# Deformable convolution and expert convolution: first offsets worked out in the head, the experts' products grouped, their neighbour rows on 64 partitions

## The chip, the cores and the metric

One core of one Trainium2 chip. The metric is the device time of one execution in microseconds, the median of several. The kernel is written in a tile language whose pools hand out buffers and insert the waits; the order of instructions on each engine is the order of the program text (a manual schedule).

## The reference

Two residual layers on x of shape (2, 256, 128, 128), float32. `_gn` normalises over 32 groups of 8 channels.

```python
def _L0(x):   # deformable 3x3 convolution, 256 -> 256 channels, here cut
    offset = conv3x3(x, w_off) + b_off          # 18 channels: dy, dx of 9 taps
    mask = sigmoid(conv3x3(x, w_mask) + b_mask) # 9 channels
    py, px = base_y + dy, base_x + dx           # for each output pixel and tap
    sampled = bilinear(x, py, px) * mask        # zero outside the image
    return einsum('bckhw,ock->bohw', sampled, w_conv) + b_conv

def _L1(x):   # 8 experts of rank 8
    h = conv(x, weight_in)     # 1x3 along a row, 256 -> 8 for each expert
    o = conv(h, weight_out)    # 3x1 down a column, 8 -> 256
    return einsum('e,ebchw->bchw', probs, o)

x = x + _L0(_gn(x))
x = x + _L1(_gn(x))
```

The eight experts together are one convolution to 64 channels (ER), a scaling by probs, and one convolution back.

## The kernel before

The normalised image is stored in DRAM as a table: one cell per pixel holds the 256 channels of the pixel and of the one below, 2 KB, with a border of zeros. A sample of one row of 128 pixels and one tap (a *unit*) is one indirect DMA of 4 KB per partition, two neighbouring cells, so all four corners at once. An image is 16 groups (`NG`) of 8 rows (`GR`), each of two chunks of 4 rows (`CR`), 9 taps: 72 units per group, 1152 per image, 2304 in all.

**Head.** x of image 0 is loaded in 16 tiles `xa` (SP queue), with `bn_stats` on VectorE as they land; then the small weights `bias`, `wu` and `bcv` are loaded. `norm_pieces` makes mean, `rstd` and `shift` (with two small matmuls by `gavg`). In a loop over the groups, `head_norm` normalises `xa` in place on ScalarE and VectorE, `transposes` turns it on TensorE, ScalarE and VectorE copy the result to `hpx` (two buffers), and `store_cells` stores 8 rows of cells, 2 MB. After the last group `offset_pieces` prepares, from rstd and shift, the scaled weights `wus` and the constant part `at` that let the offset convolution run on the raw x. Then the large weights follow on the SP queue: `wcv` (2.3 MB, L314), `win` (L315), six parts of `wout` (L319), two of `pr` (L321).

**The stream.** Everything after is laid out in *slots*, one unit each. `sched[slot]` holds the pieces that are put beside the units, and a loop over the slots emits, in this order: `gather` of unit s+15 (POOL, L491, 15 buffers), `product` of unit s+3 (ScalarE, L501: first corner times its weight into `acc`, 9 buffers), `add` of the other three corners (VectorE, L507), `apply_tap` of s-8 (TensorE, L532: one 128x512 product into `po`), `turn` of s-1 (TensorE, L517: two transposes to `ptr`), `keep` (ScalarE, L525: to `sm`), then the pieces of the slot.

The pieces are: `load_x`; `offsets_of(b, g, at_slot)`, which works out the offsets of a group from 83 slots ahead of it (`row_of` L369 into `pu`, `keep_rows` L379, `shifted` L391 into `om`, ten small VectorE steps up to `cidx` and `wt`; it reads the raw `x` tiles of its group and the next); `table_beside(1)`, which builds image 1's table beside image 0's units; and, beside image 1's units, `experts` for image 0. When a chunk's last tap is applied, `residual` (L541) adds `po` to the x tile, `result_stats` (L545) takes statistics, and `store_x1` (L548) stores the group.

For group 0 of image 0 the 83 slots lie ahead of the first unit, so `load_x`, the offset products and the small steps all come before the first gather.

**The experts.** `experts` handles 32 chunks of 4 rows. For chunk ci it loads `xc` one step ahead (L618), normalises it (`xcn`, L623) and makes `ph` on TensorE (`hidden`, L641): for each of 6 combinations of channel half and tap, one product for even rows into partitions 0 to 63 and one for odd rows into 64 to 127. These six pieces are put two slots apart. `scale` (L648) copies `ph` times probs to `h`, so that a partition half of `h` is a parity of rows. `back` (L667) then makes the 256 output channels: for each of two channel halves m six products of 128 partitions into `pe`. A product with `wout` 0 or 2 takes both row parities, two taps at once, 256 columns; the third tap lies in the row pair beside, so `wout` 1 and 3, zero in one partition half, take 128 columns each. They are put two to a slot. `total` (L676) adds `xc`, and `store` writes the output (L679). The step is 34 slots per chunk, beside image 1 and also in the *tail*, where `experts` runs for image 1 with nothing beside it. `ph`, both `pe`, `pu` and `om` share three PSUM buffers, `p_m`.

One product of float32 appears in the trace as two matmul instructions.

Of the kernel before, what the change touches and what calls it, by code (L numbers as in the profile page):

```python
# [34 lines left out]
P = 128  # L35
# [10 lines left out]
GR = 8  # L46
# [21 lines left out]
def layers(ctx, tc, x, w_om, b_om, w_cv, b_cv, w_in, w_out, probs, out):  # L68
# [45 lines left out]
    nc.vector.tensor_copy(base, base_i)  # L114

# [71 lines left out]
    def store_cells(b, j, px):  # L187

        pairs = bass.AP(
            px.tensor, px.offset, [px.ap[0], [C, GR], [1, CELL]]  # L190
        )
        nc.sync.dma_start(cells(b, GR * j - 1, GR), pairs)
# [7 lines left out]
    def offset_pieces(norm, psum, tag, name):  # L200
        mean, rstd, shift = norm
        wus = cp.tile([P, NH, NU], F32, name=f"wus_{name}")
        at = [cp.tile([P, GR, NO], F32, name=f"at{i}_{name}") for i in range(3)]
        spread = cp.tile([P, NH, P], F32, name=f"spread_{name}")
        nb = cp.tile([P, NU], F32, name=f"nb_{name}")
        by_row = cp.tile([P, 3, NO], F32, name=f"by_row_{name}")
# [52 lines left out]
    norms0, offs = [None] * B, [None] * B  # L259


    with ExitStack() as s:
        hx = s.enter_context(tc.tile_pool(name="hx", bufs=NG))
        hp = s.enter_context(tc.tile_pool(name="hpx", bufs=2))
        hs = s.enter_context(tc.tile_pool(name="hstat", bufs=1))
        ht = s.enter_context(tc.tile_pool(name="hpt", bufs=6, space=PSUM))
        h1 = s.enter_context(tc.tile_pool(name="hp1", bufs=1, space=PSUM))
        stats = hs.tile([P, NH, NCH, 6], F32, name="hstats")
        xv = view(x, 0)
        xs = []  # L270
        for g in range(NG):
            xt = hx.tile([P, NH, GN], F32, tag="hx", name=f"xa_{g}")
            nc.sync.dma_start(xt, xv[:, :, g * GN : (g + 1) * GN])
            xs.append(xt)
            for i in range(CPG):
                for h in range(NH):
                    nc.vector.bn_stats(stats[:, h, g * CPG + i], xt[:, h, i * N : (i + 1) * N])
        nc.sync.dma_start(bias, b_om.partition_broadcast(P))
        nc.sync.dma_start(wu, w_om.rearrange("p h x o -> p h (x o)"))
        nc.sync.dma_start(bcv, b_cv)  # L280
        norms0[0], pieces = norm_pieces(stats, hs, h1, "g", "0_0")
        for piece in pieces:
            piece()
        mean, rstd, shift = norms0[0]

        def head_norm(g):
            nc.scalar.activation(
                xs[g][:, 0], xs[g][:, 0], AF.Identity, bias=shift[:, 0:1], scale=rstd[:, 0:1]
            )
            nc.vector.tensor_scalar(  # L290
                xs[g][:, 1], xs[g][:, 1], mean[:, 1:2], rstd[:, 1:2], ALU.subtract, ALU.mult
            )

        px, last = None, None
        head_norm(0)
        for g in range(NG):
            px = hp.tile([P, GR + 1, C], F32, tag="hp", name=f"hpx_{g}")
            nc.gpsimd.tensor_copy(px[:, 0], last[:, GR] if g else zero[:, :C])  # L298
            if g + 1 < NG:
                head_norm(g + 1)  # L300
            for i in range(0, GR, 2):
                ps = ht.tile([P, 2, C], F32, tag="t", name=f"hpt_{g}_{i}")
                transposes(ps, xs[g], (i, i + 1))
                if i % 4 == 0:
                    nc.scalar.copy(px[:, 1 + i : 3 + i], ps)
                else:
                    nc.vector.tensor_copy(px[:, 1 + i : 3 + i], ps)
            store_cells(0, g, px)
            last = px
        store_last(0, last)  # L310
        offs[0], pieces = offset_pieces(norms0[0], h1, "g", "0")
        for piece in pieces:
            piece()
        nc.sync.dma_start(wcv, w_cv)  # L314
        nc.sync.dma_start(win, w_in)  # L315
        for i, (even, odd) in enumerate(((1, 2), (None, 0), (0, 1), (2, None))):
            for half, t in enumerate((even, odd)):
                if t is not None:
                    nc.sync.dma_start(wout[half * ER : (half + 1) * ER, i], w_out[:, t])  # L319
        for half in range(2):  # L320
            nc.sync.dma_start(pr[half * ER : (half + 1) * ER], probs)  # L321


# [3 lines left out]
    xp = pool(ctx, "x", 3)  # L327
    up = pool(ctx, "u", 1)
    ip = pool(ctx, "idx", 2)
    gp = pool(ctx, "gather", GA)  # L330
    ap = pool(ctx, "acc", 9)
    sp = pool(ctx, "sampled", 3)
    st = pool(ctx, "stat", 1)
    p_o = pool(ctx, "p_o", 1, space=PSUM)
    p_t = pool(ctx, "p_t", 3, space=PSUM)
    p_m = pool(ctx, "p_m", 3, space=PSUM)
    sides = ExitStack()
    ctx.enter_context(sides)

    sched = defaultdict(list)  # L340

    def put(slot, piece):
        sched[slot].append(piece)

    xts = {}

    def load_x(b, g):
        xt = xp.tile([P, NH, GN], F32, tag="xt", name=f"x_{b}_{g}")
        nc.sync.dma_start(xt, view(x, b)[:, :, g * GN : (g + 1) * GN])
        xts[b, g] = xt  # L350
# [4 lines left out]
    def offsets_of(b, g, at_slot):  # L355
# [4 lines left out]
        def row_of(j, i):  # L360

            if i == 0:
                held["ps", j] = p_m.tile([P, 2, C], F32, tag="m", name=f"pu_{nm}_{j}")
            y = y0 - 1 + 2 * j + i
            if not 0 <= y < H:
                return
            xt, r = xts[b, y // GR], y % GR
            for h in range(NH):
                nc.tensor.matmul(  # L369
                    held["ps", j][:, i, :NU], lhsT=xt[:, h, r * W : (r + 1) * W],  # L370
                    rhs=offs[b][0][:, h], start=(h == 0), stop=(h == NH - 1),
                )
# [28 lines left out]
        def s_pos():  # L401
            om = held["om"][:, : GR * NO].rearrange("p (r o) -> p r o", o=NO)
            at = offs[b][1][0 if g == 0 else 2 if g == NG - 1 else 1]
            nc.vector.tensor_tensor(t("pm", [P, GR, NO]), om, at, ALU.add)
# [55 lines left out]
        rows_at = [8 * j for j in range(4)] + [38]  # L460
        for j in range(5):
            put(at_slot + rows_at[j], lambda j=j: row_of(j, 0))
            put(at_slot + rows_at[j] + 3, lambda j=j: row_of(j, 1))
            put(at_slot + rows_at[j] + 6, lambda j=j: keep_rows(j))
        for n in range(9):
            put(at_slot + 45 + n, lambda n=n: shifted(n))
        put(at_slot + 55, s_pos)
        put(at_slot + 56, s_mask)
        small = (s_clamp_y, s_clamp_x, s_round, s_low, s_far, s_near, s_cell, s_index, s_masked, s_weights)
        for n, piece in enumerate(small):  # L470
            put(at_slot + 56 + n, piece)
# [79 lines left out]
    def table_beside(b):  # L551
# [40 lines left out]
        offs[b], pieces = offset_pieces(norms0[b], p_m, "m", str(b))  # L592
# [3 lines left out]
        for j in range(NG):  # L596
# [7 lines left out]
            put(slot + 42, lambda j=j: store_cells(b, j, held["px", j]))  # L604
# [215 lines left out]
```

## Time and profile before

| | us |
|---|---|
| median of 3 runs | 3915.23 (3913.02 to 3915.41) |
| the profiled execution | 3914.82 |
| its span, first to last instruction | 3912.8 |
| head, until the first `product` | 193.1 |
| tail, from the last aggregation of statistics (3677.9) | 234.9 |

| engine | busy us | share |
|---|---|---|
| TensorE, matmul (PE) | 3565.9 | 91% |
| TensorE, weight load (PEld) | 1978.3 | 51% |
| VectorE (DVE) | 3401.8 | 87% |
| ScalarE (ACT) | 1952.9 | 50% |
| GpSimd (POOL) | 2347.6 | 60% |

DMA moved 1469.56 MB, 376 GB/s on average, 1208.11 MB of it by the gathers.

In the profile's lines a line number is that of the kernel above, `out<-in` names tiles without their numbers, `xN` counts instructions, and the bracket at the end of a timeline line is how long the engine was idle before and what ended that. SP is the queue that issues ordinary DMAs. Ends of matmuls are modelled and overlap; their starts are what a cost is read from.

### The profile page before, as it was taken

The page shows a single profiled execution, that of the slowest core. Times are in us where ns is not written, and L with a number is a line of the kernel's source. Part 1 is how long each engine was busy: PE and PEld are TensorE (multiplying, and loading weights), DVE is VectorE, ACT ScalarE, POOL GpSimd, SP SyncE. Part 2 cuts the span into 40 slices and gives each one's busy share as a digit, 9 for nine tenths or more (in the row PEclk, how much of TensorE's full clock was granted, in tenths as well). Part 3 has the DMA queues.
Part 4 walks back from the last instruction along what each step waited for, and adds up shares of the span by engine and source line. Part 5 has one row for each costly group of instructions (what it writes and reads, how often), then busy time and mean ns, then how long its engine had stood idle before and what let it go on. Part 6 is the DMA issues. An engine that isn't in the chain of part 4 may idle for free.

```text
span 3912.8 us, 53037 instructions
## 1 busy us (share of the span) xinstructions
PE 3565.9 (91%) x14684; PEld 1978.3 (51%) x14684; DVE 3401.8 (87%) x7905; ACT 1952.9 (50%) x3995; POOL 2347.6 (60%) x2334
## 2 busy tenths in 40 slices
PE   2588898998888989898999999999999999999899
PEld 2444444554444544444445555555555555554576
DVE  6299999998988989899999999999999999999512
ACT  1254445555555555565555555555555555555322
POOL 0076666666666666666767666666666666667100
PEclk8699999999999999999999999999999999999999
DMA  8899999999999999999999999999999999999544
GB/s 325 322 405 409 401 389 383 389 410 407 399 412 409 397 412 401 410 406 396 408 397 397 394 397 397 389 383 375 385 381 398 399 393 395 392 395 376 194 151 146
DMA packets 433977, 1469.56 MB, mean 376 GB/s; under 512 B 41982, under 2 KB 43134, under 8 KB 433556
## 3 DMA queue, kind: packets, MB, share of 16 engines
q0 software_dynamic: 331776, 1208.11, 78.7%
q1 hardware_dynamic: 100496, 255.41, 17.3%
q8 instruction: 119, 1.95, 0.2%
q10 hardware_dynamic: 1412, 2.67, 0.2%
q14 instruction: 174, 1.43, 0.1%
HBM read 1328.61 MB, written 137.41 MB: 375 GB/s over the span
## 4 chain that ended last, share of the span: by engine, by line
PE 44%; DMA 26%; DVE 20%; issue 7%; ACT 2%; SPq 0%; POOL 0%; ACTq 0%; DVEq 0%; POOLq 0%
PE po L532 24%; DMA g<-table,cidx 21%; DVE acc L507 16%; PE ptr L517 6%; PE ph L641 4%; PE pe L667 4%; PE pu L369 4%; DMA table<-hpx 2%; DMA xc<-x 2%; PE om L391 1%; DVE stats L545 1%; DVE x L541 1%; ACT acc L501 1%; DVE tstats L563 1%; DMA table<-zero 1%
## 5 line engine op out<-in xcount | busy, mean ns | idle before, releaser
L507 DVE SCALAR_TENSOR_TENSOR acc<-g,wt,acc 128x256 f32<-128x256 f32 x6912 | 3008.2, 481 | 171.9 <-ACT acc L501 84.4
L491 POOL DMA_INDIRECT g<-table,cidx x2304 | 2337.1, 1014 | 1162.8 <-DVE acc L507 403.3
L532 PE MATMUL po<-sm,wcv 128*128 128x512 f32 x4608 | 2404.9, 604 | 120.2 <-ACT sm L525 69.1
L501 ACT ACTIVATE acc<-g,wt 128x256 f32<-128x256 f32 x2304 | 1106.4, 506 | 555.3 <-DMA g<-table,cidx 455.0
L517 PEld LDWEIGHTS ptr<-idp,acc 128*128 128x128 f32 x4608 | 613.4, 142 | 1440.1 <-issue 773.3
L525 ACT COPY sm<-ptr 128x512 f32<-128x512 f32 x1152 | 667.3, 579 | 1064.7 <-PE ptr L517 1062.3
L517 PE MATMUL ptr<-idp,acc 128*128 128x128 f32 x4608 | 906.1, 279 | 84.7 <-DVE acc L507 53.9
L532 PEld LDWEIGHTS po<-sm,wcv 128*128 128x128 f32 x4608 | 739.0, 191 | 231.6 <-ACT sm L525 84.0
L369 PE MATMUL pu<-wus,x 128*128 128x243 f32 x1264 | 315.6, 374 | 18.2 <-DMA x<-in_x_dram 18.2
L667 PE MATMUL pe<-h,wout 128*128 128x128 f32 (+1 forms) x1520 | 261.5, 312 | 0.0
L676 DVE TENSOR_TENSOR xo<-pe,xc 128x512 f32<-128x512 f32 x128 | 87.9, 687 | 189.2 <-PE pe L667 189.2
L369 PEld LDWEIGHTS pu<-wus,x 128*128 128x128 f32 x1264 | 221.4, 194 | 29.3 <-issue 17.9
L641 PE MATMUL ph<-xcn,win 128*64 128x254 f32 (+1 forms) x1536 | 220.9, 398 | 13.7 <-ACT xcn L623 12.6
L667 PEld LDWEIGHTS pe<-h,wout 128*128 128x128 f32 x1520 | 220.7, 191 | 24.9 <-issue 14.2
L391 PE MATMUL om<-u,idp 128*128 128x216 f32 (+1 forms) x576 | 154.7, 352 | 6.1 <-ACT u L379 6.1
L623 ACT ACTIVATE xcn<-xc,shift,rstd 128x512 f32<-128x512 f32 x128 | 100.8, 811 | 70.3 <-DMA xc<-x 70.3
L641 PEld LDWEIGHTS ph<-xcn,win 128*64 128x64 f32 x1536 | 89.3, 137 | 87.3 <-issue 39.3
L541 DVE SCALAR_TENSOR_TENSOR x<-po,bcv,x 128x512 f32<-128x512 f32 x128 | 95.5, 746 | 32.5 <-PE po L532 32.5
L379 ACT COPY u<-pu 128x486 f32<-128x486 f32 (+1 forms) x160 | 87.5, 547 | 34.6 <-PE pu L369 34.6
L391 PEld LDWEIGHTS om<-u,idp 128*128 128x128 f32 x576 | 88.3, 193 | 8.1 <-ACT u L379 8.1
L545 DVE BATCH_NORM_STATS2 stats<-x 128x6 f32<-128x512 f32 x128 | 87.6, 684 | 0.1
L298 POOL COPY hpx<-hpx 128x256 f32<-128x256 f32 x15 | 6.5, 435 | 133.7 <-DMA table<-hpx 73.6
(78 smaller groups left out, 590.2 us busy)
## 6 DMA issues: line engine op xcount, KB each, us to landing
g<-table,cidx POOLq DMA_INDIRECT x2304, 9.2
table<-hpx SPq DMA_DIRECT2D x16, 2048.0 KB, 9.3
x<-in_x_dram SPq DMA_DIRECT2D x32, 1024.0 KB, 9.7
x<-x SPq DMA_DIRECT2D x32, 1024.0 KB, 9.3
table<-tpx SPq DMA_DIRECT2D x16, 2048.0 KB, 18.7
xc<-x SPq DMA_DIRECT2D x64, 512.0 KB, 5.4
out_dram<-xo SPq DMA_DIRECT2D x64, 512.0 KB, 6.5
xa<-in_x_dram SPq DMA_DIRECT2D x16, 1024.0 KB, 10.6
```

What stands on the lines that cost most here:

```text
L369: nc.tensor.matmul(held["ps", j][:, i, :NU], lhsT=xt[:, h, r * W : (r + 1) * W], rhs=offs[b][0][:, h], start=(h == 0), stop=(h == NH - 1),)
L391: nc.tensor.matmul(om[:, lo:hi], lhsT=idp[:, tx : tx + P], rhs=held["u"][:, ty + lo : ty + hi, col : col + NO], start=(ty == 1 and tx == 1 ...
L491: nc.gpsimd.indirect_dma_start(out=gt[:], out_offset=None, in_=tables[b][:, :], in_offset=bass.IndirectOffsetOnAxis(ap=idx[:, rr, k : k + ...
L501: nc.scalar.activation(acc, gts[u][:, 0:C], AF.Copy, scale=wt[:, 0, rr, k : k + 1])
L507: nc.vector.scalar_tensor_tensor(accs[u], gt[:, q * C : (q + 1) * C], wt[:, q, rr, k : k + 1], accs[u], ALU.mult, ALU.add)
L517: nc.tensor.transpose(pts[u // 2][:, h, (r % 2) * W : (r % 2 + 1) * W], acc[:, h * P : (h + 1) * P], ident)
L525: nc.scalar.copy(sms[u // CR][:, :, (r - 1) * W : (r + 1) * W], pts.pop(u // 2))
L532: nc.tensor.matmul(pos_[b, ci, m], lhsT=wcv[:, h, k, m * P : (m + 1) * P], rhs=sms[u // CR][:, h], start=(k == 0 and h == 0), stop=(k == K ...
L541: nc.vector.scalar_tensor_tensor(v, pos_.pop((b, ci, m)), bcv[:, m : m + 1], v, ALU.add, ALU.add)
L545: nc.vector.bn_stats(stats1[b][:, m, ci], xts[b, ci // CPG][:, m, at_ : at_ + N])
L641: nc.tensor.matmul(o[:, :, to], lhsT=win[:, h, tap], rhs=rows[:, t, :, of], start=(n == 0), stop=(n == 5),)
L667: nc.tensor.matmul(ps[m].rearrange("p (j t x) -> p t j x", t=2, x=W)[:, t, to], lhsT=l, rhs=hs[c].rearrange("p (j x) -> p j x", x=W)[:, of ...
```

## The change

Five parts.

1. **Group 0's offsets in the head.** `offsets_of` now returns its pieces with their slots. For group 0 of image 0 it is given the normalised tiles `xs`, the unscaled weights `wu` and a constant `plain` (base and bias), which need nothing of `offset_pieces`. Its 36 pieces are run four at a time after the stores of groups 2 to 10 of the head's loop. `load_x` and `offset_pieces` stay, after the loop, for the groups that follow.
2. **Weights earlier.** `wcv`, `win`, `wout` and `pr` are loaded right after `bcv`, ahead of the norm.
3. **First stores.** In group 0 of the head, cells are stored two rows at a time, as soon as they are copied. The transposes have four PSUM buffers in place of six, since `p_m` exists from the head on.
4. **The experts.** All 12 products of `hidden` come in one slot. `back` makes the 128-partition products of both row parities (t) into two PSUM tiles, each holding both channel halves. `back_beside` makes the eight neighbour products in one slot, with 64 partitions of `wout` and `h` in place of 128 with zeros: t = 0 reads partitions 64 to 127, t = 1 reads 0 to 63, in turns. `total` goes by t, with rows interleaved. The step is 33 slots beside image 1.
5. **The tail.** All pools of the stream are closed first; the experts then have 8 PSUM buffers and 8, 3, 4 and 4 of `xc`, `xcn`, `h` and `xo`. Pieces are ordered with a step of 24, and `xc` is loaded six chunks ahead.

```diff
-        ht = s.enter_context(tc.tile_pool(name="hpt", bufs=6, space=PSUM))
+        ht = s.enter_context(tc.tile_pool(name="hpt", bufs=4, space=PSUM))
...
         nc.sync.dma_start(bcv, b_cv)
+        nc.sync.dma_start(wcv, w_cv)
+        nc.sync.dma_start(win, w_in)
+        for i, (even, odd) in enumerate(((1, 2), (None, 0), (0, 1), (2, None))):
...
+        nc.vector.tensor_tensor(
+            plain, base, bias.unsqueeze(1).broadcast_to([P, GR, NO]), ALU.add
+        )
+
+        samples = [piece for _, piece in offsets_of(0, 0, (xs, wu, plain))]
...
-            store_cells(0, g, px)
+                if g == 0:
+                    store_cells(0, g, px, i, 2)
+            if g > 0:
+                store_cells(0, g, px, 0, GR)
+            if g > 1:
+                for piece in samples[:4]:
+                    piece()
+                del samples[:4]
...
-        def hidden(ci, n):
+        def hidden(ci):
+
+            ps["h"] = psum.tile([P, 512], F32, tag=tag, name=f"ph_{b}_{ci}")
+            for n, (h, tap) in enumerate(((0, 1), (1, 1), (0, 0), (1, 0), (0, 2), (1, 2))):
...
+        def back(ci, m):
+
+            for t in range(2):
+                if m == 0:
+                    ps[t] = psum.tile([P, NH, N // 2], F32, tag=tag, name=f"pe_{b}_{ci}_{t}")
+                nc.tensor.matmul(
+                    ps[t][:, m], lhsT=wout[:, 2 * t, m * P : (m + 1) * P], rhs=hs[ci],
+                    start=(m == 0), stop=False,
+                )
+
+        def back_beside(ci):
+            last = {0: 1, 1: 1 if ci + 1 < NCH else 0}
+            for m in range(NH):
+                for j in range(2):
+                    for t, c, i in ((0, ci - 1 + j, 1 - j), (1, ci + j, 1 - j)):
+                        if not 0 <= c < NCH:
+                            continue
+                        half = slice(ER, P) if t == 0 else slice(0, ER)
+                        nc.tensor.matmul(
+                            ps[t][:, m, j * W : (j + 1) * W],
+                            lhsT=wout[half, 1 + 2 * t, m * P : (m + 1) * P],
+                            rhs=hs[c][half, i * W : (i + 1) * W],
+                            start=False, stop=(m == NH - 1 and j == last[t]),
+                        )
...
         for ci in range(NCH + 1):
             e = first + step * ci
             if ci < NCH:
-                put_(e - step, lambda ci=ci: load(ci))
+                put_(e - ahead, lambda ci=ci: load(ci))
...
-                for n in range(6):
-                    put_(e + 5 + 2 * n, lambda ci=ci, n=n: hidden(ci, n))
-                put_(e + 18, lambda ci=ci: scale(ci))
+                put_(e + 6, lambda ci=ci: hidden(ci))
+                put_(e + 9, lambda ci=ci: scale(ci))
             if ci > 0:
                 c = ci - 1
                 for m in range(NH):
-                    n_parts = len(parts(c, m))
-                    for n in range(n_parts):
-                        put_(e + 20 + 5 * m + n // 2, lambda c=c, m=m, n=n: back(c, m, n))
-                    put_(e + 27 + 5 * m, lambda c=c, m=m: total(c, m))
-                put_(e + 33, lambda c=c: store(c))
+                    put_(e + 12 + 3 * m, lambda c=c, m=m: back(c, m))
+                put_(e + 18, lambda c=c: back_beside(c))
+                for t in range(2):
+                    put_(e + 20 + 2 * t, lambda c=c, t=t: total(c, t))
+                put_(e + 23, lambda c=c: store(c))
...
-        pools = expert_pools(sides, 0)
-        experts(0, norms1[0], pools, p_m, "m", put, slot + 36, 34)
+        pools = expert_pools(sides, 3, 2, 4, 2)
+        experts(0, norms1[0], pools, p_m, "m", put, slot + 36, 33, 33)
...
-    sides.close()
-    pools = expert_pools(sides, 0)
+    stream.close()
+    p_m = pool(ctx, "p_e", 8, space=PSUM)
+    pools = expert_pools(ctx, 8, 3, 4, 4)
     tail = defaultdict(list)
-    experts(1, norms1[1], pools, p_m, "m", lambda slot, piece: tail[slot].append(piece), 0, 34)
+    experts(1, norms1[1], pools, p_m, "e", lambda slot, piece: tail[slot].append(piece), 0, 24, 24 * 6)
```

## The prediction

> **What bounds the kernel now.** I read the stage table first (columns: span, then busy time and count of PE, PEld, DVE, ACT, POOL, then granted TensorE clock, DMA share, GB/s).
>
> ```profile
> 160.00:165.00 5.00, 0.00 (x0) 0.00 (x0) 0.00 (x0) 0.00 (x0) 0.00 (x0) 0.50 0.72 227
> 185.00:190.00 5.00, 3.75 (x19) 3.15 (x17) 2.72 (x11) 0.83 (x2) 1.16 (x1) 1.00 0.00 0
> ...
> 2014.00:2114.00 100.00, 94.18 (x356) 48.37 (x356) 97.44 (x233) 53.72 (x116) 71.13 (x71) 1.00 1.02 402
> 3014.00:3114.00 100.00, 100.00 (x422) 56.61 (x421) 96.03 (x226) 53.26 (x114) 68.11 (x68) 1.00 1.02 399
> ...
> 3700.00:3800.00 100.00, 95.98 (x696) 72.50 (x695) 20.05 (x29) 28.20 (x43) 0.00 (x0) 1.00 0.49 154
> ```
>
> Four regimes. Until 155 us the head is bound by the table stores (DMA share 1.03, 380 GB/s). From 155 to 193 us a chain of latencies runs with DMA partly empty. The stream follows; in its second image, beside the experts, PE is at 98.6% (mean of 1914 to 3614 us), DVE at 95.0%. The last 235 us (the tail) are PE alone. The timeline of the head's end:
>
> ```profile
> 164.28 1.10 SPq L321 DMA_DIRECT2D pr<-in_probs_dram  x2
> 165.50 1.03 SPq L349 DMA_DIRECT2D x<-in_x_dram  x2
> ...
> 171.05 10.28 PE L369 MATMUL pu<-wus,x 128*128 128x243 f32 x36 [17.76 <-DMA x<-in_x_dram]
> ...
> 188.00 0.46 DVE L453 TENSOR_TENSOR wt<-nf 128x288 f32<-128x288 f32 x1
> 188.62 1.16 POOL L491 DMA_INDIRECT g<-table,cidx  x1 [43.49 <-DVE wt L453]
> ...
> 193.12 0.51 ACT L501 ACTIVATE acc<-g,wt 128x256 f32<-128x256 f32 x1 [5.35 <-DMA g<-table,cidx]
> ```
>
> SP issues the weights before it issues x; PE waits for x, and POOL for the indices. Then PE's timeline inside the second image, to price an expert piece:
>
> ```profile
> 2730.02 0.38 PE L517 MATMUL ptr<-idp,acc 128*128 128x128 f32 x2
> 2730.24 1.02 PE L532 MATMUL po<-sm,wcv 128*128 128x512 f32 x2
> 2731.09 0.38 PE L517 MATMUL ptr<-idp,acc 128*128 128x128 f32 x2
> 2731.41 0.65 PE L641 MATMUL ph<-xcn,win 128*64 128x256 f32 x4
> 2731.99 1.13 PE L532 MATMUL po<-sm,wcv 128*128 128x512 f32 x2
> 2732.95 0.38 PE L517 MATMUL ptr<-idp,acc 128*128 128x128 f32 x2
> ```
>
> Starts tell the cost, since ends overlap. A unit (ptr and po) takes 2731.09 - 2730.02 = 1.07 us; one with a `hidden` piece 2732.95 - 2731.09 = 1.86. The piece costs 0.78 us. Consecutive 512-column instructions start 0.43 us apart, so 256 columns stream in 0.213 and 128 in 0.107. The piece's four instructions of 256 columns, on two 64-column halves, therefore overlap in pairs (0.43 us), and 0.35 is the change of array shape, there and back. The tail, one chunk:
>
> ```profile
> 3748.62 3.78 PE L667 MATMUL pe<-h,wout 128*128 128x256 f32 x24
> ...
> 3752.32 2.80 PE L641 MATMUL ph<-xcn,win 128*64 128x256 f32 x24
> ...
> 3755.05 3.78 PE L667 MATMUL pe<-h,wout 128*128 128x256 f32 x24
> ...
> 3758.09 1.52 ACT L623 ACTIVATE xcn<-xc,shift,rstd 128x512 f32<-128x512 f32 x2 [2.45 <-DMA xc<-x]
> ```
>
> This period is 6.43 us. Streaming alone is 12 x 0.213 = 2.56 for `hidden` plus 8 x 0.213 + 16 x 0.107 = 3.41 for `back`, so two shape changes cost 0.46, 0.23 each. Over the tail the period is (3901.37 - 3693.72)/30 = 6.92 us: 0.5 us goes to waiting for `xcn`, itself waiting for `xc`.
>
> **Head.** The weight loads (2.95 MB, ten issues, about 9.5 us of SP) move ahead of the norm. SP is free from 41.0 us, so they are issued by 50.6; DMA moved 1 GB/s from 52 to 62 us, and 2.95 MB at 400 GB/s need 7.4 us. Cost nothing; if that cover failed, they would cost 7.4 us of stores. The first group's two-row stores start when ACT's copy at 61.90 ends (62.5) instead of 65.06; the 33.8 MB then land near 152.5 rather than 155. The 36 pieces of group 0's offsets go between the groups' copies, four per group, from group 2 to 10. Their work is that of 171 to 188 us, about 17 us, of which PE 14. DVE and ACT waited for stores in 51.7 and 49.6 us of the head, about 3 us in each group; a stall of a piece in an engine's queue lies in there (uncovered it would cost up to 17). Fewer PSUM buffers for transposes, 4 for 6, still hold one group.
>
> So gathers wait for the stores alone: issued at 153, landed 4.5 us later as at 193.12, or 9 later at the stream's median of 8.8 to 9.6 under load. The stream starts 31 to 36 us earlier. Not all is kept: x of groups 0 and 1 and two loads for the table beside (4 MB, 10 us of DMA) used to run before the gathers and now run among them, and DVE at 97.4% (200 to 300 us) cannot catch up. I take **-25** (bounds -15 and -34).
>
> **Second image.** Before, per chunk of 34 slots: `hidden` 6 x 0.78 = 4.68, `back` 3.50 (its groups take 0.65, 0.66 and 0.44, per half), together 8.18, 0.241 a slot. After, per 33 slots: `hidden` in one place 2.56 + 0.41 (two changes, between 0.35 and 0.46) = 2.97. `back` on 128 partitions 8 x 0.213 = 1.71. The neighbours on 64 partitions: 16 instructions of 128 columns, a shape that no row shows. If the two halves overlap as `hidden`'s do, 0.86; if not, 1.73, the present price. The nearest row is `hidden`'s, but that overlaps with weights of 64 columns, and these have 128; I count half the overlap, 1.29, plus a new pair of changes, 0.41. Sum 2.97 + 1.71 + 1.29 + 0.41 = 6.38, 0.193 a slot: 0.047 x 1056 slots = 50 us of PE. But DVE is next. The stores of the result are the stream's beat, one per group of 72 units: 13 groups beside the experts take 3576.15 - 2172.41 = 1403.7 us, 108.0 each; the last group before them takes 2172.41 - 2069.42 = 103.0, with DVE at 97.4%. The experts' own work on DVE, two `total`s of 0.69 us a chunk, 2.2 chunks a group, adds some 2.7: at best 105.7, so 2.3 x 14.7 groups = 34 us can be had. With two engines nearly full and PE working in lumps of 3 us I take three quarters: **-26** (bounds -8 and -34).
>
> The Trainium skill (TensorE: Matmul & The Clock Gate, LDWEIGHTS) says that a weight load takes time by its columns and not by its contraction length, 32x128 the same as 128x128. By it the 16 loads of 128 columns alone would fill 1.7 us and the halving of partitions would gain nothing; the sum would be that of the first rival. Its page TensorEngine Tiling (Array Packing), Key Properties, says that tiles load and multiply in parallel, which would give 0.86. No run here shows yet which holds for row halves.
>
> **Stream's end.** With 34 slots the last chunk overran the stream: two `total`s (1.27 us at 3675.19) and one more stood before the aggregation at 3677.91, though its statistics ended at 3675.27. With 33 slots the chunks end inside: **-2.5**.
>
> **Tail.** Loads six chunks ahead take away the wait for `xc`. Period: 2.56 + 1.71 + 1.29 + three changes 0.70 = 6.26, against 6.92: 0.66 x 31 = **-20** (bounds -34 with full overlap, 0 if something else refills it). The strided `total` has the same 512 elements as the present one (691 ns, two per chunk), ACT needs 2 x 0.81 + 0.47 us per chunk: both idle enough.
>
> The profiled execution took 3914.82 us, 2.0 more than its span and 0.4 under the median. 3914.8 - 25 - 26 - 2.5 - 20 = **3841 us**.
>
> **Rivals.** *No overlap of the halves* (0.2): expert price (2.97 + 1.71 + 1.73 + 0.41)/33 = 0.207, 36 us of PE, close to DVE's 34, so -23; tail period 6.70, -7; in all 3857. *Second image held by DVE and DMA* (0.15): nothing there, 3867. For it: DMA share 1.00 throughout, DVE at 97.4% before the experts begin. Against it: ACT waits only 7.7 us for gathers between 1950 and 3600, while it waits 770 us for PE. *The early start is paid back* (0.12): the offsets are not ready or the loads starve the gathers, head -10, in all 3856. *Slower* (0.08): three `p_m` buffers serve `ph`, both `pe` halves (now held together from slot e+12 to e+22) and the offsets' `pu` and `om`; PE is in order, so a `pe` that waits for an `om` to be read stops all units behind it, while the lumps drain DVE's lead. `product` runs ahead of `turn` by five slots' worth of `acc` buffers, some 7 us, which speaks against. The longest such waits today are 2.8 us (DVE for `po`) and 3.0 us (ACT for `ptr`). At 3 us a chunk, 32 x 3 = 96 us lost, against 47.5 won elsewhere: 3963. It turns slower above 1.5 us a chunk.
>
> **Numbers.** Forecast 0.45, the rest as given. 0.2% (8 us) is about what a measurement of this kernel can tell from no change. All but the last case are faster by more: 0.92; of the last I put 0.06 slower and 0.02 inside. The range goes from all the good bounds (-34 - 34 - 2.5 - 34, 3810, rounded down to 3808) to 3882, past the rivals at 3856 to 3867 with a weaker head.
>
> **What would show it.** Right: first gather near 153 us and DMA never empty after 62; `hidden` bursts of 24 in about 3 us; PE below 98% and DVE at 97% or more beside the experts; 16 neighbour instructions in 0.9 to 1.3 us; tail period near 6.3. Wrong: neighbours at 1.7 or above, PE waiting for `om` or `xo` in the second image, or DVE idle behind `po` once a chunk.

## The result, and the profile after

| | before, us | after, us |
|---|---|---|
| median of 4 runs | 3915.09 (3913.02 to 3915.41) | 3828.78 (3827.25 to 3829.05) |
| profiled execution / its span | 3914.82 / 3912.8 | 3828.66 / 3826.8 |

The ratio is 0.978 (95% interval 0.9763 to 0.9797). The span fell by 86.0 us; the forecast was 74. The sum holds in total, its terms less so:

| stage, read from | before | after | change | forecast |
|---|---|---|---|---|
| start to the sixteenth x1 store (the second image, image 1, starts) | 1965.58 | 1938.57 | -27.0 | -25 |
| from there to the last x1 store | 1709.0 | 1688.4 | -20.6 | -26 |
| last x1 store to the final aggregation | 3.34 | 0.62 | -2.7 | -2.5 |
| aggregation to the end of the span | 234.9 | 199.25 | -35.6 | -20 |

The stores of x1 (SP, L548 before and L564 after, one per group of 72 units) are the stream's beat. Their shift was already -25.2 us at the first store (320.57 to 295.33), -27.0 at the sixteenth and -47.6 at the last (3674.57 to 3626.93), so each stage can be separated by subtraction.

The stage table of after, columns as in the prediction (span, then busy time and count of PE, PEld, DVE, ACT, POOL, granted TensorE clock, DMA share, GB/s):

```profile
50.00:62.00 12.00, 2.33 (x10) 2.19 (x11) 9.15 (x20) 2.68 (x4) 0.00 (x0) 1.00 0.81 291
...
2160.00:3560.00 1400.00, 1368.16 (x5877) 761.23 (x5874) 1337.24 (x3143) 744.18 (x1579) 954.54 (x947) 1.00 1.01 395
3640.00:3820.00 180.00, 179.57 (x1490) 126.39 (x1491) 39.87 (x62) 57.84 (x93) 0.00 (x0) 1.00 0.51 163
```

The stretch beside the experts in the kernel before:

```profile
2160.00:3560.00 1400.00, 1390.04 (x5785) 770.07 (x5785) 1321.58 (x3101) 729.81 (x1561) 939.39 (x931) 1.00 1.00 389
```

The weights fill the hole of the head: 291 GB/s where the same stretch of before moved 49. Beside the experts PE is now at 1368.16/1400 = 97.7% (before 1390.04, 99.3%) and DVE at 95.5% (before 1321.58, 94.4%). In the tail PE hardly waits any more (179.57 of 180).

The head's end, from the timeline of all engines:

```profile
156.06 1.16 POOL L507 DMA_INDIRECT g<-table,cidx  x1 [13.32 <-issue]
...
158.49 1.99 PE L289 MATMUL pu<-wus,x 128*128 128x243 f32 x4 [7.59 <-DMA x<-in_x_dram]
...
163.20 0.56 ACT L299 COPY u<-pu 128x486 f32<-128x486 f32 x1 [19.84 <-PE pu L289]
...
163.76 0.51 ACT L517 ACTIVATE acc<-g,wt 128x256 f32<-128x256 f32 x1
...
166.32 0.51 ACT L517 ACTIVATE acc<-g,wt 128x256 f32<-128x256 f32 x1 [2.05 <-DMA g<-table,cidx]
...
169.02 0.51 ACT L517 ACTIVATE acc<-g,wt 128x256 f32<-128x256 f32 x1 [2.20 <-DMA g<-table,cidx]
```

The first gather goes out at 156.06 and waits for no index. The first `product` is at 163.76 in place of 193.12, 29.4 us earlier. Ahead of it in ACT's queue stands a piece of group 1's offsets (`u<-pu`), which waits for PE, and PE for x. Whether it held the product up is open: the shortest time from issue to landing of a gather between 150 and 180 us is 7.7 us, and 156.06 + 7.7 is 163.76. The products after it wait for their gathers. Some 4 us are given back by the first store (-25.2).

DVE's waits in the second image, 2160 to 3560 us (columns: total us, times, longest):

```profile
DVE xo L699 <- PE pe L685: 22.3, 14, 3.5
DVE x L557 <- PE po L548: 6.6, 7, 2.1
```

Before, the same list was:

```profile
DVE x L541 <- PE po L532: 28.7, 17, 2.8
DVE acc L507 <- ACT acc L501: 10.4, 17, 1.3
DVE pm L404 <- PE om L391: 5.8, 8, 0.8
```

Those 44.9 us have shrunk to 6.6, but a wait that was not in the list, of `total` for the neighbours' products, takes 22.3.

The tail, PE's timeline:

```profile
3723.78 1.99 PE L670 MATMUL pe<-h,wout 128*128 128x256 f32 x8
3725.70 1.16 PE L685 MATMUL pe<-h,wout 64*128 64x128 f32 x16
3726.80 2.80 PE L656 MATMUL ph<-xcn,win 128*64 128x256 f32 x24
3729.52 1.99 PE L670 MATMUL pe<-h,wout 128*128 128x256 f32 x8
```

The period is 3729.52 - 3723.78 = 5.74 us, against a mean of 6.92 before. The sixteen neighbour instructions with the shape change after them take 3726.80 - 3725.70 = 1.10 us.

### The profile page after: what moved, and what is told of

The parts are those of the page before. It is cut to its first block, busy times and chain, and to the rows that moved or that the text cites. A ratio compares the mean times of both kernels' runs of the same rounds, so it can differ in the third digit from the quotient of the medians.

```text
span 3826.8 us, 53039 instructions
## 1 busy us (share of the span) xinstructions
PE 3489.7 (91%) x14684; PEld 1929.2 (50%) x14684; DVE 3394.8 (89%) x7906; ACT 1952.6 (51%) x3995; POOL 2350.2 (61%) x2334
## 3 DMA queue, kind: packets, MB, share of 16 engines
q1 hardware_dynamic: 100544, 255.41, 17.6%
## 4 chain that ended last, share of the span: by engine, by line
PE 38%; DMA 28%; DVE 23%; issue 8%; ACT 1%; POOL 0%; SPq 0%; ACTq 0%; DVEq 0%; POOLq 0%
DMA g<-table,cidx 25%; PE po L548 20%; DVE acc L523 19%; PE ptr L533 6%; PE ph L656 4%; PE pu L289 3%; PE pe L670 3%; DMA table<-hpx 2%; PE pe L685 1%; DVE x L557 1%; DVE stats L561 1%; ACT acc L517 1%; PE om L311 1%; DVE tstats L579 1%; DMA table<-zero 1%
## 5 line engine op out<-in xcount | busy, mean ns | idle before, releaser
L548 PE MATMUL po<-sm,wcv 128*128 128x512 f32 x4608 | 2398.0, 602 | 128.5 <-ACT sm L541 68.5
L548 PEld LDWEIGHTS po<-sm,wcv 128*128 128x128 f32 x4608 | 746.6, 192 | 187.6 <-ACT sm L541 81.3
L656 PE MATMUL ph<-xcn,win 128*64 128x254 f32 (+1 forms) x1536 | 181.1, 385 | 4.4 <-ACT xcn L639 4.4
L656 PEld LDWEIGHTS ph<-xcn,win 128*64 128x64 f32 x1536 | 105.3, 138 | 62.0 <-issue 7.6
L670 PE MATMUL pe<-h,wout 128*128 128x256 f32 x512 | 129.5, 385 | 0.0
L663 ACT ACTIVATE h<-ph,pr 128x256 f32<-128x256 f32 x64 | 30.4, 475 | 148.8 <-PE ph L656 148.8
L670 PEld LDWEIGHTS pe<-h,wout 128*128 128x128 f32 x512 | 90.7, 190 | 20.5 <-issue 11.8
```

The lines of the kernel that those rows point to most:

```text
L548: nc.tensor.matmul(pos_[b, ci, m], lhsT=wcv[:, h, k, m * P : (m + 1) * P], rhs=sms[u // CR][:, h], start=(k == 0 and h == 0), stop=(k == K ...
L656: nc.tensor.matmul(o[:, :, to], lhsT=win[:, h, tap], rhs=rows[:, t, :, of], start=(n == 0), stop=(n == 5),)
L670: nc.tensor.matmul(ps[t][:, m], lhsT=wout[:, 2 * t, m * P : (m + 1) * P], rhs=hs[ci], start=(m == 0), stop=False,)
```

## The experiments

Times are medians of several executions; where one run is named, it is a single execution. The kernel before was measured again beside each set of experiments, and its median lay between 3912.94 and 3915.09 us, so a difference between medians of different sets is sure to some 2 us. The x1 stores in the traces tell smaller differences.

**1. The head alone** (experts and tail as before). Does the early start last to the end?

```diff
-        experts(0, norms1[0], pools, p_m, "m", put, slot + 36, 33, 33)
+        experts(0, norms1[0], pools, p_m, "m", put, slot + 36, 34)
```

(`experts`, its pools and the tail's lines are those of before.)

> The head of the changed kernel with the experts and the tail of the kernel before. Theory (the four gains add up and the head's is its own): the stream starts 27 us earlier and nothing else moves, so 3915 - 27 = 3888 us, with x1 stores of image 1 still 108.0 us apart and the tail still 235 us. Rival (the early start is paid back later, because the stream is held by DMA over its whole length): the 27 us shrink along image 0 and 1, 3895 to 3915 us.

Measured 3884.11 us (before 3913.74; ratio 0.9924, interval 0.9908 to 0.9941). Every x1 store from the sixteenth (1938.55) to the last (3647.62, before 3674.57) is 27.0 us early. The start is not paid back. The whole came out 4 us below the 3888 expected, which lies in the tail: it took 234.4 us from the last store, before 238.2; with the same code, its mean period came out at 6.79 us in place of 6.92. Why the same code ran faster there is open. DVE's waits in the second image are those of before, 29.0 + 10.1 + 5.8 = 44.9.

**2. Weights late** (they follow the head's stores, as before; offsets still in the head).

```diff
-        nc.sync.dma_start(wcv, w_cv)
-        nc.sync.dma_start(win, w_in)
...
         store_last(0, last)
+        nc.sync.dma_start(wcv, w_cv)
+        nc.sync.dma_start(win, w_in)
...
```

> The changed kernel with wcv, win, wout and pr loaded after the last table store, as before, ahead of x. Theory (in the head only the empty DMA time of 52 to 62 us made them free): 2.95 MB, 7.4 us of DMA, and 9.5 us of SP issue stand between the stores and x; gathers don't wait for them, so they come among the gathers with x: the stream's beat is 7 to 12 us later, 3836 to 3841 us. Rival (the offsets of group 0 no longer wait for x, so weights after the stores are hidden too): 0 to 2 us, 3829 to 3831 us.

Measured 3841.84 us, ratio to before 0.9819 (0.9802 to 0.9835). The first x1 store came at 309.02, 13.7 us after that of the changed kernel, and the last 12.7 later. The timeline of this kernel:

```profile
149.40 6.63 SPq L459 DMA_DIRECT2D wout<-in_w_out_dram  x6
155.93 1.16 POOL L507 DMA_INDIRECT g<-table,cidx  x1 [13.36 <-issue]
...
165.11 1.40 SPq L486 DMA_DIRECT2D x<-in_x_dram  x2
...
176.42 1.99 PE L289 MATMUL pu<-wus,x 128*128 128x243 f32 x4 [25.69 <-DMA x<-in_x_dram]
...
183.38 0.56 ACT L299 COPY u<-pu 128x486 f32<-128x486 f32 x1 [40.18 <-PE pu L289]
183.84 2.90 ACT L517 ACTIVATE acc<-g,wt 128x256 f32<-128x256 f32 x7
```

The gathers are issued on time (155.93), and their data lie ready: seven products then run in a row. What is late is x, whose issue stands behind the weights on SP (165.11 in place of 147.05). PE waits for x, and ACT, in order, waits for PE ahead of its first product. So the weights' place is worth more than their bytes (2.95 MB, 7.4 us at 400 GB/s), because of what is queued behind them.

**3. First group stored whole.**

```diff
-                if g == 0:
-                    store_cells(0, g, px, i, 2)
-            if g > 0:
-                store_cells(0, g, px, 0, GR)
+            store_cells(0, g, px, 0, GR)
```

> The changed kernel with the first group's cells stored as a whole, not two rows at a time. Theory (the stores give the beat of the head, so their start is its start): the first store comes 2.5 us later and all stores with it, stream's beat 2.5 us later: 3831 us. Rival (the head catches up, since its stores queue two deep): no change, 3829 us.

One run, 3830.97 us. The first store of the head starts at 64.76 in place of 62.61, and the first x1 store at 297.55, 2.2 us later. The first gather goes out at 158.40, 2.3 us later than in after, so it follows the stores. The two-row stores give what they advance.

**4. Neighbours on 128 partitions again** (the halves with zeros; order, slots and pools as after).

```diff
-                        half = slice(ER, P) if t == 0 else slice(0, ER)
+                        half = slice(0, P)
```

> The changed kernel, but the neighbour products read all 128 partitions of wout and h (half of wout is zero there), as before. Theory (two halves of 64 partitions run at once): the 16 instructions take 1.71 us instead of 0.86, and one change of array shape per chunk is saved: tail period 2.56 + 3.41 + 0.46 = 6.43 instead of 5.75 us, tail 21 us longer; in image 1 0.5 us more of PE per chunk, 0 to 16 us in all: 3850 to 3866 us. Rival (the tail gained from the loads ahead and the grouping, not from the halves): tail period about 6.0 or less, 3829 to 3837 us.

Measured 3859.10 us, ratio to before 0.9862 (0.9845 to 0.9878): 30.3 us slower than after. The tail, PE's timeline:

```profile
3744.20 1.95 PE L685 MATMUL pe<-h,wout 128*128 128x128 f32 x16
3746.08 2.80 PE L656 MATMUL ph<-xcn,win 128*64 128x256 f32 x24
...
3750.64 1.61 PE L685 MATMUL pe<-h,wout 128*128 128x128 f32 x13
```

Sixteen instructions with the shape change behind them take 1.88 us in place of 1.10, and the period is 3750.64 - 3744.20 = 6.44. The tail is 20.7 us longer and the second image 9.7, so the step to 64 partitions is worth 30 us. Whether that is because two halves run at once, or because a product on 64 partitions is cheaper, experiment 5 tells.

This run also shows what the early loads of the tail, with their buffers, are worth without the cheaper products. With the neighbours at their old price its tail takes 220.0 us from the aggregation, 14.9 less than the 234.9 of before, and its period of 6.44 is the 6.43 that the prediction gave for a chunk of before that waits for nothing.

**5. One half after the other** (four products of t = 0, then four of t = 1, all on 64 partitions).

```diff
-            for m in range(NH):
-                for j in range(2):
-                    for t, c, i in ((0, ci - 1 + j, 1 - j), (1, ci + j, 1 - j)):
+            for t in range(2):
+                for m in range(NH):
+                    for j in range(2):
+                        c, i = (ci - 1 + j, 1 - j) if t == 0 else (ci + j, 1 - j)
```

> The changed kernel with the eight neighbour products in another order: first the four that read partitions 64 to 127, then the four that read 0 to 63. Theory (the gain comes from two halves running at once, which needs neighbours in the queue to be on different halves): 16 instructions take 1.71 us, tail period 6.6 us, tail 26 us longer, image 1 5 to 25 us longer: 3860 to 3880 us. Rival (an instruction on 64 partitions is cheaper by itself, with a shorter weight load): nothing changes, 3829 us, neighbours still 1.1 us.

One run, 3849.03 us. PE's timeline in the tail:

```profile
3741.17 1.99 PE L670 MATMUL pe<-h,wout 128*128 128x256 f32 x8
3743.09 1.71 PE L686 MATMUL pe<-h,wout 64*128 64x128 f32 x16
3744.73 2.80 PE L656 MATMUL ph<-xcn,win 128*64 128x256 f32 x24
```

The time falls between the theory (3860 to 3880 us) and the rival (3829). The stretch takes 1.64 us: 0.54 more than in turns, 0.24 less than on 128 partitions (1.88). Starts of single instructions, read from the timeline in narrow windows, say where both come from. Inside one half an instruction starts every 0.11 us, as on 128 partitions, so 64 partitions are not cheaper by themselves. In after the instructions of the two halves start in pairs, 0.01 us apart (3725.70 and 3725.71, later 3726.25 and 3726.26). In this run the first half starts from 3743.09 to 3743.98 and the second from 3743.65 to 3744.53: they overlap at the seam even in this order, which saves about two starts, and that is the 0.24.

**6. `hidden` spread again** (six pieces of two products in slots e+5 to e+10; the tail as after). Is it worth anything to have them in one place?

```diff
-                put_(e + 6, lambda ci=ci: hidden(ci))
-                put_(e + 9, lambda ci=ci: scale(ci))
+                for k in range(6):
+                    put_(e + 1 + k if step == 24 else e + 5 + k, lambda ci=ci, k=k: hidden(ci, k))
+                put_(e + 9 if step == 24 else e + 11, lambda ci=ci: scale(ci))
```

> The changed kernel with hidden again in six pieces, one per slot beside image 1 (the tail's order on TensorE is unchanged). Theory (each piece pays 0.35 us for two changes of array shape): 6 x 0.78 = 4.68 instead of 2.97 us per chunk, 1.7 us more of PE, 0.052 per slot, which takes PE from about 1.43 to 1.48 us a slot and so past VectorE: image 1 10 to 25 us longer, 3839 to 3854 us. Rival (in image 1 VectorE and DMA bound anyway, so PE's saving is idle, and the lump of 3 us even hurts): no change or up to 10 us faster, 3819 to 3830 us.

Measured 3868.98 us, ratio to before 0.9887 (0.987 to 0.9903). The last x1 store is 39.6 us later than in after, the tail unchanged (200.1 and 199.9 us from the last store). This missed on both sides: more than any theory gave, and the stream is 18.9 us slower than with the experts of before (experiment 1, 3666.52 against 3647.62), whose pieces lay two slots apart. PE's timeline in a chunk:

```profile
2994.83 0.38 PE L533 MATMUL ptr<-idp,acc 128*128 128x128 f32 x2
2995.14 0.65 PE L657 MATMUL ph<-xcn,win 128*64 128x256 f32 x4
2995.72 1.12 PE L548 MATMUL po<-sm,wcv 128*128 128x512 f32 x2
2996.68 0.38 PE L533 MATMUL ptr<-idp,acc 128*128 128x128 f32 x2
```

A unit with a piece takes 2996.68 - 2994.83 = 1.85 us, six in a row, while DVE's three adds per unit at 481 ns (the mean in the table of groups) need 1.44. Shape changes cost 6 pairs in place of one, about 5 x 0.35 = 1.75 us a chunk, or 56 us over 32 chunks, of which 39.6 show. That the closer spacing is what makes it worse than the experts of before fits this timeline (there a unit of 1.07 us lies between two of 1.86, and DVE can catch up), but no run moved the spacing alone, so it stays open.

**7. `total` three slots later** (image 1 alone; the tail's slots kept). Is the new wait what the second image lost?

```diff
-                    put_(e + 20 + 2 * t, lambda c=c, t=t: total(c, t))
-                put_(e + 23, lambda c=c: store(c))
+                    put_(e + 23 + 2 * t if step > 24 else e + 20 + 2 * t, lambda c=c, t=t: total(c, t))
+                put_(e + 26 if step > 24 else e + 23, lambda c=c: store(c))
```

> The changed kernel with both totals three slots later beside image 1 (e+23 and e+25 in place of e+20 and e+22, store at e+26), five slots behind the neighbour products as a whole. Theory (VectorE stops 22 us in image 1 because total comes two slots after the products that it reads, while TensorE is behind): those waits go, image 1 10 to 20 us shorter, 3809 to 3819 us. Rival (the PSUM buffers are now held longer, and TensorE waits for them instead): waits of TensorE for total or for offsets' tiles of 10 to 30 us, 3826 to 3845 us. Third (VectorE and DMA give the beat anyway): 3825 to 3830 us.

Measured 3818.06 us, ratio to before 0.9759 (0.9743 to 0.9776), 10.7 us faster than after. DVE's waits, same window:

```profile
DVE x L557 <- PE po L548: 16.7, 15, 2.9
DVE acc L523 <- ACT acc L517: 0.9, 3, 0.4
```

The wait for the neighbours is gone; part of it comes back at `po`, the next point where DVE runs into PE.

**8. The lumps spread as well** (beside image 1: `hidden` at e+4, `back` at e+15 and e+17, neighbours at e+20, totals as in 7; step 24 is the tail, as after).

```diff
-                put_(e + 6, lambda ci=ci: hidden(ci))
+                put_(e + 6 if step == 24 else e + 4, lambda ci=ci: hidden(ci))
...
-                    put_(e + 12 + 3 * m, lambda c=c, m=m: back(c, m))
-                put_(e + 18, lambda c=c: back_beside(c))
+                    put_(e + 12 + 3 * m if step == 24 else e + 15 + 2 * m, lambda c=c, m=m: back(c, m))
+                put_(e + 18 if step == 24 else e + 20, lambda c=c: back_beside(c))
```

> The changed kernel with the pieces of a chunk spread over its 33 slots beside image 1: hidden at e+4, back at e+15 and e+17, neighbours at e+20, totals at e+23 and e+25 (before: e+6, e+12, e+15, e+18, e+20, e+22). Theory (TensorE has on average 0.2 us of room per slot, and 6 us of products within 12 slots put it 3 us behind, so VectorE waits): spreading removes that, 10 to 25 us shorter, 3804 to 3819 us, and better than moving the totals alone. Rival (waits for PSUM buffers take their place): as in the run with later totals, 3826 to 3845 us. Third (VectorE and DMA give the beat anyway): 3825 to 3830 us.

Measured 3813.13 us, ratio 0.9744 (0.9728 to 0.976). DVE's waits:

```profile
DVE x L557 <- PE po L548: 8.5, 11, 2.0
DVE pm L324 <- PE om L311: 2.1, 2, 1.3
DVE xo L699 <- PE pe L685: 1.6, 2, 1.1
```

Thirteen groups beside the experts take (3514.41 - 2144.96)/13 = 105.3 us each, 0.4 below the 105.7 that the prediction gave as DVE's best. DVE is at 1353.5/1400 = 96.7%.

The second image of all these kernels follows one sum, DVE's listed waits between 2160 and 3560 us:

| kernel | DVE's waits | against after | last x1 store against after |
|---|---|---|---|
| old experts (1) | 44.9 | +16.0 | +20.7 |
| hidden spread (6) | 64.0 | +35.1 | +39.6 |
| neighbours on 128 (4) | 37.5 | +8.6 | +9.7 |
| half by half (5) | 31.4 | +2.5 | +3.4 |
| after | 28.9 | | |
| totals later (7) | 17.6 | -11.3 | -11.5 |
| spaced (8) | 12.2 | -16.7 | -16.0 |

The change in DVE's waits gives the change in time to within 5 us. Almost all of them are waits for PE (experiments 1 and 6 have 10.1 and 13.0 us for ACT among them). This is close to bookkeeping: DVE does the same work in each version, and its idle time beyond the listed waits is 33 to 34 us of the 1400 in all of them. What is not bookkeeping is that moving pieces moves the waits (7 and 8). PE's own busy share does not tell it: it is 97.7% in after and 98.3% in the faster kernel 8.

**9. The tail with loads one chunk ahead** (and `xc`, `xcn`, `h`, `xo` with 3, 2, 4, 2 buffers).

```diff
-    pools = expert_pools(ctx, 8, 3, 4, 4)
+    pools = expert_pools(ctx, 3, 2, 4, 2)
...
-    experts(1, norms1[1], pools, p_m, "e", lambda slot, piece: tail[slot].append(piece), 0, 24, 24 * 6)
+    experts(1, norms1[1], pools, p_m, "e", lambda slot, piece: tail[slot].append(piece), 0, 24, 24)
```

> The changed kernel with xc in the tail loaded one chunk ahead, and with the buffers of before (3, 2, 4, 2). Theory (the loads ahead took away the waits for xc that cost 0.5 us of each 6.92 us period): they come back, period 6.1 to 6.3 instead of 5.75 us, ScalarE waits for xc some 30 to 70 us again, tail 11 to 17 us longer: 3840 to 3846 us. Rival (loads that run freely behind fewer other pieces land in time anyway): period 5.75, 3829 us.

One run, 3865.90 us: the tail took 236.9 us from the last store in place of 199.9. That is more than expected (3840 to 3846 us), and nearly all of the tail's gain. The waits of this kernel, 3640 to 3860 us:

```profile
ACT xcn L639 <- DMA xc<-x: 68.1, 27, 4.5
...
PE ph L656 <- ACT xcn L639: 26.2, 26, 2.9
```

The mean period is 5.74 + 37.0/31 = 6.94 us, the 6.92 of before, although PE works 0.7 us less per chunk than it did then. By these waits it is the chain of load, normalisation and products that sets the period here, not PE. The run moved the loads and took the buffers back in one step, so which of the two does it is not separated. Together with experiment 4, the tail from the aggregation takes 234.9 us in before, 236.3 with the cheaper products but not the early loads, 220.0 with the early loads but not the cheaper products, and 199.25 with both. So the early loads stand by themselves, and the cheaper products are worth nothing without them.

**10. The tail in pairs of chunks** (two chunks' `hidden`, then two of `back`, then two of neighbours; 10, 4, 6, 4 buffers).

```diff
             e = first + step * ci
+            if step == 24:
+                e = step * (ci - ci % 2) + ci % 2
...
-    pools = expert_pools(ctx, 8, 3, 4, 4)
+    pools = expert_pools(ctx, 10, 4, 6, 4)
```

(The tiles of a chunk are kept by its number, since two chunks are open at once.)

> The changed kernel with the tail's chunks taken in pairs: hidden of two chunks, then back of two, then the neighbours of two, with 10, 4, 6 and 4 buffers. Nothing is left out. Theory (the tail is TensorE alone, 5.13 us of streaming and 0.61 us for three changes of array shape per chunk): half the changes go, period 5.44 instead of 5.75 us, 31 x 0.3 = 9 us shorter: 3819 to 3821 us. Rival (the 0.61 us are the fill of each group of products and not the change of shape, or waits for xcn take their place): 3826 to 3832 us.

Measured 3821.91 us (before 3913.30; ratio 0.9766, 0.9752 to 0.9781), 6.9 us faster than after. PE's timeline:

```profile
3724.97 5.37 PE L656 MATMUL ph<-xcn,win 128*64 128x256 f32 x48
3730.28 3.72 PE L670 MATMUL pe<-h,wout 128*128 128x256 f32 x16
3733.93 2.06 PE L685 MATMUL pe<-h,wout 64*128 64x128 f32 x32
3735.91 1.30 PE L656 MATMUL ph<-xcn,win 128*64 128x256 f32 x10
```

One chunk takes (3735.91 - 3724.97)/2 = 5.47 us, 0.27 less, with 1.5 shape changes in place of 3: 0.18 each. The 32 neighbour instructions with the change behind them take 3735.91 - 3733.93 = 1.98 us, so sixteen more cost 0.88.

**11. Spaced and in pairs** (8 and 10 together).

> Both improvements together: the pieces of a chunk spread over 33 slots beside image 1 and the tail in pairs. Nothing is left out. If they are independent, 3829 - 16 - 9 = 3804 us (3802 to 3807). If the tail in pairs gains nothing, 3812 to 3814 us.

Measured 3805.68 us (3805.17 to 3807.05, five runs; before 3913.30), ratio 0.9726 (0.9713 to 0.9739). The two gains add: 3828.8 - 15.7 - 6.9 = 3806.2. This version beats both kernels.

## Why the prediction was right, and where it was mis-sized

**Head: the theory held, -27 for -25.** Group 0's offsets hide in the head's waits: the table stores are issued over 81.5 us, before over 81.4, while the waits of DVE and ACT for them (62 to 156 us) shrink from 51.7 and 49.6 us to 46.3 and 43.4. The gathers wait for the stores (experiment 3), and experiment 1 shows the gain at every later store, so "the early start is paid back" falls. Of the 29.4 us won at the first product some 4 are lost until the first store: the second to fifth products wait 2.0 to 2.7 us each for their gathers, before 0.9 to 1.6. That fits the loads of x that now run among the gathers, as the working said; no run moved these alone. The working missed the end of the stores: the last is issued at 145.70 and lands 9.3 us later, at 155.0, not 152.5, and the gather goes out at 156.06, not 153. The early weights, costed only as 7.4 us of bytes at worst, are worth 13.7 at the first store (experiment 2), the two-row stores 2.2 (experiment 3). The rest of the 25.2 falls to the offsets by subtraction only, since no run took them alone out of the head.

**Second image: "three quarters of 34" was too much, -20.6 for -26.** PE's saving was real and DVE was next, as the sum had it. Redone with its own figures the bound is 106.0 and not 105.7 us per group (2.2 chunks of two `total`s of 0.69 us are 3.0, not 2.7); experiment 8 goes below either, to 105.3. The mis-sized step is the discount. It was a guess for lumps in general, and it did not see one particular wait: `total` stands two slots behind the neighbours it needs, and PE, which has just been through its lumps, has not come to them when DVE has. From the timeline of all engines:

```profile
2984.60 6.13 DVE L523 SCALAR_TENSOR_TENSOR acc<-g,wt,acc 128x256 f32<-128x256 f32 x14
...
2991.96 1.16 PE L685 MATMUL pe<-h,wout 64*128 64x128 f32 x16
...
2993.15 0.69 DVE L699 TENSOR_TENSOR xo<-pe,xc 128x512 f32<-128x512 f32 x1 [2.42 <-PE pe L685]
```

Experiment 7 wins back 11.5 us by moving it alone, experiment 8 16.0 by moving the lumps too. This is the mechanism of the "slower" rival in a mild form (DVE stopped by PE once in a while), by `xo`, not by `p_m`: no wait of PE for `om` or for `xo` appears. The delay goes both ways, though: PE in turn waits for DVE to empty `po`, 9.1 us in the same window, before 0.5 and in experiment 8 1.6.

```profile
PE po L548 <- DVE x L557: 9.1, 13, 1.2
```

"DVE at 97% or more" was wrong, 95.5%, for the same reason.

**Stream's end: -2.7 for -2.5.** The chunks end inside the stream, as worked out.

**Tail: -35.6 for -20, a term mis-sized, and outside its own bound of -34.** The step was "I count half the overlap, 1.29". The halves overlap entirely: in after both start their eight instructions in the time in which one half alone does in experiment 5 (0.89 us from the first start to the last). The stretch of 1.10 us with a shape change in it splits into the 0.86 of the lower bound and 0.24; experiment 10 gives 0.88 for the sixteen. Streaming is 2.56 + 1.71 + 0.86 = 5.13, and 5.74 - 5.13 = 0.61 is left for the three changes, counted as 0.70. The two errors are 0.43 + 0.09 = 0.52 us a period, x 31 = 16 us, which is the whole miss. The half was a mean between two mechanisms, and no row spoke for the mean. The nearest row (`hidden`, whose halves overlap in pairs) had said which, though its halves are of columns and these of rows. That the wait of 0.5 us goes was right, and experiment 4 shows it by itself: 6.92 to 6.44. What the sum did not say is that the cheaper products need it: in experiment 9, without the early loads, the tail is 37 us longer, which is 1.2 us a period and not 0.5.

Of the two rules weighed there, the one on LDWEIGHTS was taken for a bound on the whole stretch. The Trainium skill, TensorE: Matmul & The Clock Gate, LDWEIGHTS (loading the stationary operand), says that load time goes by columns alone. One load agrees with that: its median in the tail is 188 ns on 64 partitions and 192 on 128. Sixteen loads one behind the other, 1.7 us by an estimate from that page's figure, are not what happened: the stretch takes 1.10 in turns and 1.88 on 128 partitions (experiment 4). The Trainium skill, TensorEngine Tiling (Array Packing), Key Properties, has tiles load and multiply in parallel, and that agrees with the paired starts. The same section says that a change of tiling mode drains the engine. The tail shows a cost of 0.18 to 0.2 us for each change of shape (experiment 10, and 0.61/3); that it is a drain no run here shows.

**The total** was forecast as 3841 and measured as 3828.8, 12 us less. That is in part luck: the gain was 2.0 us larger than forecast in the head, 5.4 smaller in the second image and 15.6 larger in the tail, and the middle one hid a part of the last. Of the rivals, "no overlap" is shown false by experiments 4 and 5, and "held by DVE and DMA" half true: DVE is the next limit, but 20.6 us could be had before it. Whether DMA (400 GB/s, share 1.02) is what holds experiment 8 where it is was not separated from DVE.

## What to carry to other kernels

Where two engines are nearly full, place each consumer behind its producer by the time the producer's engine needs to get there, not by a count of slots that looks safe: here three slots on one piece were worth 11 us. The sum of VectorE's waits told each version's time in the second image to within 5 us, which its own or TensorE's busy share did not. When the price of a new shape is one of two mechanisms, take the one that the nearest row shows and give the other a chance of its own; here the mean had no row behind it. Two gains on the same loop need not add: cheaper products gave nothing while the loads were late, the early loads gave 14.9 us alone, and both together 35.6.

## What the runs showed of the hardware

Products on 64 partitions whose row halves alternate run two at a time: the sixteen instructions of 128 columns start in pairs 0.01 us apart, a pair every 0.11 us, and all start within 0.89 us. On 128 partitions one starts every 0.11 us, and all within 1.67 us. Inside one half one starts every 0.11 us as well, so an instruction on half the partitions is not cheaper; with one half after the other all start within 1.44 us, because the second half begins before the first is through. Of the 0.78 us between 128 partitions and halves in turns, 0.54 hang on the order of issue, which I had not expected at that size. A change of array shape costs about 0.2 us, so a piece of 0.43 us that stands alone between other shapes costs 0.78.
